# The last values made among attention's first scores, the exponentials' buffers moved, and a second norm queued behind the first turning

## The chip, the cores and the metric

The kernel runs on one core of a Trainium2 chip. A core has five engines that run side by side, each taking its own instructions in order: TensorE (PE; its weight loads are listed apart as PEld), VectorE (DVE), ScalarE (ACT), GpSimd (POOL) and SyncE (SP), which here only issues DMAs. They work on SBUF, 128 partitions of on-chip memory. TensorE writes to PSUM, eight banks of 128 partitions by 512 float32 values.

The metric is the time on the device, in microseconds, of one execution of the whole kernel. Times before and after are medians of several runs. A profile is one further execution, taken with the hardware profiler.

## The reference, cut to what matters

N = 4096 rows of width D = 256 pass through two layers. Layer 0 is a graph attention applied twice; layer 1, where all of the change lies, is a transformer block with 8 heads of 32 and a mask from `adj`:

```
# layer 0: two graph attentions with elu and residuals        (not touched)
# layer 1:
qkv    = layer_norm(x, g1, be1) @ w_qkv          # 4096 x 768: queries, keys, values
scores = einsum('nhd,mhd->hnm', q, k) * 32**-0.5
attn   = softmax(where(adj != 0, scores, -inf))
out    = einsum('hnm,mhd->nhd', attn, v).reshape(n, 256)
x      = x + out @ w_proj + b_proj
h2     = layer_norm(x, g2, be2)
x      = x + gelu(h2 @ w1 + b1) @ w2 + b2        # w1: 256 x 1024
```

## The kernel before, in words

Layer 1 is `unshifted_transformer`. It has three stages, and takes the rows in 8 blocks of 512 (`NB`), each of four tiles of 128 (`TB`).

**The projection** (lines 1782 to 1853, some 11.2 us per block) goes through the blocks `nb`. It transposes the next block's normed rows (L1556) and copies them out of PSUM with gain and bias (L1559); makes keys and then queries, two column tiles each (L1810); splits each result into a float16 head (the cast on ScalarE, L1817) and a float16 rest (the subtraction on VectorE, L1818) in a tile `u_halves`, which two DMAs store to `half_d` (L1822); and makes the block's values (L1829), which ScalarE copies to `u_v` (L1836). Then it loads keys of an earlier block from `half_d` into the layout that attention wants (L1734): the keys' heads go in twice and their rests twice, either all four by DMA (blocks from `NNB - 3` on) or two by DMA and two by a VectorE copy (L1846). The order of SP's queue is as written here; that of the other engines in this stage is made by a planner from the order of the program and its own estimates of when operands are ready. The SBUF pools `u_hv` (3 halves tiles) and `u_x` (5 tiles of rows) and a PSUM pool of all eight banks are opened for this stage. The weights `w_qkv` lie in `g_adj` tiles at the right end of SBUF, the normed and turned rows `g_ft` beside them; these two pools (stage and rows) are closed behind the projection (`pools.close()`).

**Attention** (lines 1876 to 2113) goes through 512 units (block of queries, group of four heads, tile of 128 keys), each in two steps `u` of two heads. A step's `weights` makes eight score matmuls into one of three two-bank PSUM tiles `u_ps` (L1872), the exponential in place on ScalarE (L1882), and the product with the mask on VectorE into `u_e` (L1883), one of ten buffers of the pool `u_work`. One step in 32 leaves the product to GpSimd. Two units later (`weigh`) TensorE multiplies the products with the values into `u_av`; GpSimd adds pairs of products into `u_both`, six more buffers of the same pool, and TensorE sums those four units later (`total`) into `u_dn`. These two are queued as parts in `waiting`, from which each step takes three or four behind its scores. Here all five engines' orders are as written: a stalled instruction holds everything behind it on its engine.

**The end of attention** is a table `ending`: by unit and step, what to do there. `project(k)` multiplies the first two blocks' attention with `w_proj` (L2048), adds it to the rows (L2056), takes the norm's moments (L1514, L1521, the root on ScalarE L1526), normalises (L1535, L1543) and adds `b2` on GpSimd (L2065). `turn_first(c)` transposes half of block 0's normed rows into `u_av` (L1556), and ScalarE copies them out (L1559).

**The feed-forward stage** goes through the eight blocks: 32 matmuls for `w1` (L2186) with Gelu on ScalarE (L2193), the projection of a later block (L2147), the next block's transposes, and 64 matmuls for `w2` (L2206). TensorE's order is as written.

A pool opened in the place of a closed one makes its first users wait until the closed pool's last users are done.

Of the kernel before, what the change touches and what calls it, by code (L numbers as in the profile page):

```python
# [22 lines left out]
P = 128  # L23
# [1544 lines left out]
class Ahead:  # L1568
# [26 lines left out]
    def normed(self, nb):  # L1595
        self.norms.normed(self.xs[nb], self.xs[nb], self.held.pop(nb))

    def turned(self, nb, c, pt):
        if c == 0:
            self.hn[nb] = self.stage_p.tile([P, self.D // P, 512], F32, name="g_ft", tag="stage")  # L1600
        self.norms.turned(self.hn[nb], c, self.xs[nb], pt, 1)

# [31 lines left out]
def unshifted_transformer(  # L1634
# [85 lines left out]
    with ExitStack() as scope:  # L1720
# [59 lines left out]
                load()  # L1780

        with ExitStack() as qkv:
            hv = qkv.enter_context(tc.tile_pool(name="u_hv", bufs=3))
            ps_q = qkv.enter_context(tc.tile_pool(name="u_ps_q", bufs=8, space=PSUM))
            u_x = qkv.enter_context(tc.tile_pool(name="u_x", bufs=5))
            wq_sb = ahead.w

            qkv.enter_context(tc.manual_schedule(engines={mybir.EngineType.SP}))
            for nb in range(3, 6):
                ahead.load(nb, u_x)  # L1790
            for nb in range(NNB):
                cols = slice(nb * NB, (nb + 1) * NB)
                hn = ahead.hn.pop(nb)
                if nb == 1:
                    for later_nb in range(6, NNB):
                        ahead.load(later_nb, u_x)
                if nb + 1 < NNB:
                    for c in range(DC):
                        ahead.turned(nb + 1, c, ps_q.tile([P, NB], F32, name="misc"))
                if 2 < nb + 2 < NNB:  # L1800
                    ahead.moments(nb + 2)
                    if nb + 3 == NNB:
                        nc.scalar.activation(rooted, ahead.held[nb + 2][:, 0, 1:2], AF.Exp)
                    ahead.normed(nb + 2)
                for i in (1, 0):
                    halves = hv.tile([P, 2, DC, NB], F16, name="u_halves")
                    for c in range(DC):
                        pq = ps_q.tile([P, NB], F32, name="misc")
                        for k in range(DC):
                            nc.tensor.matmul(  # L1810
                                pq,
                                wq_sb[k][:, i * D + c * P : i * D + (c + 1) * P],
                                hn[:, k, :],
                                start=(k == 0),
                                stop=(k == DC - 1),
                            )
                        nc.scalar.copy(halves[:, 0, c, :], pq)  # L1817
                        nc.vector.tensor_tensor(  # L1818
                            halves[:, 1, c, :], pq, halves[:, 0, c, :], op=ALU.subtract
                        )  # L1820
                    for kind in range(2):
                        nc.sync.dma_start(  # L1822
                            half_d[i, kind, :, :, cols].rearrange("c p n -> p c n"),
                            halves[:, kind],
                        )
                for t in range(TB):
                    pv = ps_q.tile([P, NB], F32, name="misc")
                    for k in range(DC):
                        nc.tensor.matmul(  # L1829
                            pv[:, :D],  # L1830
                            hn[:, k, t * P : (t + 1) * P],
                            wq_sb[k][:, 2 * D : 3 * D],
                            start=(k == 0),
                            stop=(k == DC - 1),
                        )
                    nc.scalar.copy(v_sb[:, nb * TB + t, :], pv[:, :D])  # L1836

                for b in (nb - 1,) if nb + 1 < NNB else (nb - 1, nb):
                    if b >= 0:
                        at = slice(b * NB, (b + 1) * NB)  # L1840
                        for c in range(DC):
                            late = b >= NNB - 3
                            kinds = (0, 0, 1, 1) if late else (0, None, 1, None)
                            stack(k_st[c][:, :, at], 1, kinds, at, c, HC)
                            for o in () if late else (0, 2 * O):
                                nc.vector.tensor_copy(  # L1846
                                    k_st[c][o + O : o + 2 * O, :, at], k_st[c][o : o + O, :, at]
                                )
                    if b == 0:
                        load_queries(0)  # L1850
                if 2 <= nb < 2 + NT // MC:
                    load_chunk(0, nb - 2)
        pools.close()


        work = scope.enter_context(tc.tile_pool(name="u_work", bufs=10))
        tail = scope.enter_context(tc.tile_pool(name="u_tail", bufs=1))
        ps_s = scope.enter_context(tc.tile_pool(name="u_ps_s", bufs=3, space=PSUM))
        ps_a = scope.enter_context(tc.tile_pool(name="u_ps_a", bufs=1, space=PSUM))
# [52 lines left out]
        def weigh(nb, c, mt, es, part):  # L1912
            if mt == 0 and part == 0:
                sums_of["av"] = ps_a.tile([P, NB], F32, name="u_av")
            h = c * HC
            lefts = [v_sb[:, mt, (h + j) * O : (h + j + 1) * O] for j in range(HC)]
            four(sums_of["av"], lefts, es, part, mt == 0, mt == NT - 1)
            if mt == NT - 1 and part == PARTS - 1:
                num = tail.tile([P, NB], F32, name="u_num", bufs=2)
                nc.scalar.copy(num, sums_of["av"])  # L1920
                nc.sync.dma_start(att_d[c, :, nb * NB : (nb + 1) * NB], num)

        def alone(mt):
            return mt // 2 % 8 == 7
# [89 lines left out]
        def rows_ready(k):  # L2014
# [8 lines left out]
                lambda: rows_ready(1),  # L2023
                lambda: nc.scalar.activation(rooted, norms.eps, AF.Sqrt),
                lambda: project(0),
            ],
            (last + 3, 0): [lambda: project(1)],
            (last + 3, 1): [lambda: turn_first(0)],
            (last + 4, 1): [lambda: turn_first(1)],
        }  # L2030

        def ready(step, i, es):
# [9 lines left out]
        def project(k):  # L2042
            res, att = early[k][:2]
            pp = ps_s.tile([P, 2, NB], F32, name="u_ps").rearrange("p a (b d) -> p (a b) d", d=D)
            per = TB // 2
            for t in range(TB):
                for c in range(DC):
                    nc.tensor.matmul(  # L2048
                        pp[:, t, :],
                        att[:, c, t * P : (t + 1) * P],  # L2050
                        early["wp"][:, c, :],
                        start=(t % per == 0 and c == 0),
                        stop=(t % per == per - 1 and c == DC - 1),
                    )
            for t in range(TB):
                nc.vector.tensor_tensor(res[:, t, :], res[:, t, :], pp[:, t, :], op=ALU.add)  # L2056
            both = norms.moments(res)
            if k == 0:
                two = blocks.tile([P, 2, TB * D], F32, name="u_q")
                res_n = two[:, 0].rearrange("p (t d) -> p t d", t=TB)  # L2060
                early["hn"] = two[:, 1].rearrange("p (c n) -> p c n", c=DC)
            else:
                res_n = masks.tile([P, TB, D], F32, name="u_mask")
            norms.normed(res_n, res, both)
            nc.gpsimd.tensor_tensor(  # L2065
                res, res, early["b2"].to_broadcast([P, TB, D]), op=ALU.add
            )
            early[k] = res, res_n

        def turn_first(c):  # L2070
            norms.turned(
                early["hn"], c, early[0][1], ps_a.tile([P, NB], F32, name="u_av"), 2
            )
        scope.enter_context(tc.manual_schedule(engines=ordered))
        for i in range(len(units) + 5):
            for u in range(HC // 2):
                if i < len(units):
# [8 lines left out]
                    if u == 0:  # L2086
                        pace()
                    es_of.setdefault(i, []).append(weights(*units[i], u))
                    if u == 0 and i + 2 < len(units) and units[i + 2][2] % 16 == 0 and (
                        units[i + 2] != (NNB - 1, DC - 1, NT // 2)  # L2090
                    ):
                        keep_mask(*units[i + 2])
                    if i % 2 == 1 and not alone(mt):
                        both = work.tile([P, 2, NB], F32, name="u_both", bufs=6)
                        nc.gpsimd.tensor_tensor(both, es_of[i - 1][u], es_of[i][u], op=ALU.add)  # L2095
                        both_of.setdefault(i, []).append(both)
                if u == 0 and 0 <= i - 2 < len(units):
# [18 lines left out]
    with ExitStack() as scope:  # L2116
# [43 lines left out]
        def turned(res_n):  # L2160
            hn = ln.tile([P, DC, NB], F32, name="ln_cols")
            for c in range(DC):
                norms.turned(hn, c, res_n, bank(), 2)
            return hn
# [162 lines left out]
```

## Time and profile before

| | |
|---|---|
| median of 3 runs | 3123.89 us (3123.82 to 3124.47) |
| the profiled execution | 3124.94 us on the device |
| its span, first to last instruction | 3123.2 us |
| mean granted TensorE clock | 0.995 of full |
| projection, first to last matmul | about 1601.7 to 1690.6 us of the span |
| attention, first score to last exponential | 1693.0 to 2850.8 us |
| feed-forward, from its first matmul | from 2865.9 us |

A page of the profile gives each engine's busy time, the chain of work that ended last (followed back from the end, from each instruction to what released it), and groups of instructions: line, engine, operation, output <- inputs, count, busy time and mean duration, and the idle time of the engine ahead of them with what ended it. Times of a timeline or chain are microseconds from the span's start. In a table by stretches, each engine has its busy microseconds and instruction count; the last three columns are the TensorE clock that was granted (1.00 is full), the DMA engines' busy share, and GB/s. Matmuls overlap, and the profile models their ends, so a busy TensorE need not be one at its peak.

### The profile page before, as it was taken

To read this page: it belongs to the slowest core of one execution; us is meant where nothing else is said; L and a number is where in the kernel's file an instruction comes from. 1 tells how busy PE (TensorE), PEld (TensorE's weight loads), DVE (VectorE), ACT (ScalarE), POOL (GpSimd) and SP (SyncE) were. 2 spreads that over 40 slices of the span, in tenths; PEclk is the share of its full clock that TensorE was granted. 3 is DMA by queue.
4 is the path that set the end of the run, shared out by engine and by line. 5 is a ranking of instruction groups with operands and counts; after the bars stand their busy time and mean duration, and the time that the engine had idled before them with its cause. 6 is when DMAs were issued, how large, how long until landed. Compare 5 with 4: busy or idle time off the path is not lost.

```text
span 3123.2 us, 139201 instructions
## 1 busy us (share of the span) xinstructions
PE 3061.6 (98%) x63976; PEld 2713.3 (87%) x63976; DVE 2747.7 (88%) x3110; ACT 2699.7 (86%) x3370; POOL 1265.1 (41%) x568
## 2 busy tenths in 40 slices
PE   6999999999999999999999999999999999999998
PEld 5899999999889999999975888888888888887766
DVE  7999999999989999999985999999999999997220
ACT  6899999999899999999975999999999999996232
POOL 3300000000330000000002999999999999997110
PEclk8999999999999999999999999999999999999999
DMA  8666555431311213121145101010101110013210
GB/s 257 218 198 205 171 174 167 144 100 33 91 59 29 90 56 97 32 64 53 46 116 152 34 21 35 21 41 28 35 21 35 30 30 28 28 40 102 68 34 22
DMA packets 213171, 250.35 MB, mean 80 GB/s; under 512 B 89120, under 2 KB 133664, under 8 KB 212576
## 3 DMA queue, kind: packets, MB, share of 16 engines
q1 hardware_dynamic: 212576, 241.37, 25.1%
q8 instruction: 502, 8.22, 1.1%
q14 instruction: 93, 0.76, 0.1%
HBM read 198.84 MB, written 42.47 MB: 77 GB/s over the span
## 4 chain that ended last, share of the span: by engine, by line
PE 51%; ACT 1%; DVE 1%; issue 0%; DMA 0%; DVEq 0%; ACTq 0%
PE u_ps L1872 15%; PE u_av L1904 14%; PE u_dn L1904 8%; PE misc L2186 4%; PE misc L2206 4%; PE bank L1463 3%; PE misc L1810 2%; PE misc L1829 1%; ACT t L1122 1%; PE misc L2147 1%; PE misc L1556 0%; DVE t L1137 0%; DVE t L1124 0%; DVE u_e L1883 0%; PE u_ps L2048 0%
## 5 line engine op out<-in xcount | busy, mean ns | idle before, releaser
L1463 PE MATMUL bank<-vst,t 128*128 128x132 f16 x16384 | 1455.9, 220 | 3.6 <-DVE t L1137 2.7
L2095 POOL TENSOR_TENSOR u_both<-u_e 128x1024 f32<-128x1024 f32 x448 | 1047.9, 2388 | 805.1 <-DMA u_k<-half_d 775.6
L1463 PE MATMUL bank<-vst,mask 128*128 128x132 f16 (+1 forms) x10516 | 1372.3, 206 | 0.0
L1122 ACT ACTIVATE t<-s_b,g_terms 128x1024 int8<-128x1024 f32 x1234 | 1318.7, 1148 | 21.0 <-PE bank L1463 15.2
L1463 PEld LDWEIGHTS <-t 128*128 128x128 fp8e4 x16384 | 1186.3, 96 | 15.8 <-DVE t L1137 5.4
L1883 DVE SCALAR_TENSOR_TENSOR u_e<-u_mask,u_ps 128x1024 f32<-128x1024 uint8 x994 | 1131.5, 1213 | 26.8 <-ACT u_ps L1882 25.8
L1882 ACT ACTIVATE u_ps<-u_ps 128x1024 f32<-128x1024 f32 x994 | 996.4, 1008 | 93.0 <-PE u_ps L1872 33.6
L1463 PEld LDWEIGHTS <-mask 128*128 128x128 fp8e4 x10516 | 920.4, 98 | 0.0
L1137 DVE SCALAR_TENSOR_TENSOR t<-mask,t 128x2048 int32<-128x2048 int32 x256 | 587.9, 2296 | 74.8 <-ACT t L1122 66.4
L1872 PE MATMUL u_ps<-u_q,u_k 128*32 128x512 f16 x8192 | 632.4, 381 | 7.0 <-DVE u_e L1883 4.5
L1904 PE MATMUL u_av<-u_e,u_v 128*32 128x128 f32 x16384 | 602.9, 273 | 0.0
L1124 DVE TENSOR_SCALAR t<-s_b,g_terms 128x1024 fp8e4<-128x1024 f32 x814 | 590.1, 758 | 2.7 <-DMA s_b<-s_d 2.7
L1904 PEld LDWEIGHTS u_av<-u_e,u_v 128*32 128x32 f32 x16384 | 483.2, 110 | 120.6 <-issue 0.7
L1054 POOL TENSOR_TENSOR vst<-g_adj,vst 128x528 f16<-128x528 f32 x16 | 19.9, 1241 | 725.7 <-ACT g_big L1018 681.6
L1904 PE MATMUL u_dn<-u_both,u_ones 128*32 128x128 f32 x7168 | 279.2, 273 | 0.0
L1904 PEld LDWEIGHTS u_dn<-u_both,u_ones 128*32 128x32 f32 x7168 | 212.9, 110 | 52.1 <-issue 0.7
L1872 PEld LDWEIGHTS <-u_k 128*32 128x32 f16 x8192 | 229.5, 96 | 29.2 <-issue 8.9
L2193 ACT ACTIVATE u_hid<-misc,n_b 128x512 f32<-128x512 f32 x64 | 43.9, 687 | 140.3 <-PE misc L2186 140.3
L2206 PE MATMUL misc<-u_k,u_hid 128*128 128x256 f32 x512 | 111.8, 379 | 0.0
L2206 PEld LDWEIGHTS misc<-u_k,u_hid 128*128 128x128 f32 x512 | 96.7, 190 | 13.3 <-issue 0.5
L2186 PE MATMUL misc<-ln_cols,u_k 128*128 128x512 f32 x224 | 97.3, 592 | 0.0
L867 DVE TENSOR_SCALAR adj<-g_adj 128x1024 fp8e4<-128x1024 int32 x123 | 88.9, 723 | 3.8 <-DMA g_adj<-in_adj_dram 3.8
(186 smaller groups left out, 1919.2 us busy)
## 6 DMA issues: line engine op xcount, KB each, us to landing
g_adj<-in_adj_dram SPq DMA_DIRECT2D x123, 512.0 KB
s_b<-s_d SPq DMA_DIRECT2D x64, 512.0 KB
mask<-mask SPq DMA_DIRECT2D x128, 256.0 KB
u_mask<-mask SPq DMA_DIRECT2D x64, 256.0 KB
mask<-stage SPq DMA_DIRECT2D x48, 256.0 KB
half_d<-u_halves SPq DMA_DIRECT2D x32, 256.0 KB
u_q<-half_d SPq DMA_DIRECT2D x32, 256.0 KB
rows<-e_x SPq DMA_DIRECT2D x31, 256.0 KB
```

Of the source, the lines that this page charges most:

```text
L867: nc.vector.tensor_scalar(v.rearrange("p m r -> p r m"), loaded.pop((nb, c, i)), 1.0, -(2.0**-30), op0=ALU.min, op1=ALU.max, saturate=False,)
L1122: nc.scalar.activation(to.bitcast(I8), s, AF.Sign, bias=negd, scale=-1.0)
L1124: nc.vector.tensor_scalar(to, s, negd, -1.0, op0=ALU.is_ge, op1=ALU.mult, saturate=False)
L1137: nc.vector.scalar_tensor_tensor(both, m32.unsqueeze(1).to_broadcast(list(both.shape)), SIGNS, both, op0=ALU.bitwise_or, op1=ALU.bitwise_and,)
L1463: nc.tensor.matmul(to, left, right, start=k not in opened, stop=last)
L1872: nc.tensor.matmul(ps[r * O : (r + 1) * O, j, :], k_st[c][:, 2 * u + j, at : at + O], q_st[:, h, :], start=True, stop=True,)
L1882: nc.scalar.activation(ps, ps, AF.Exp, scale=SCALE)
L1883: nc.vector.scalar_tensor_tensor(e, mask, 0.0, ps, op0=ALU.not_equal, op1=ALU.mult)
L1904: nc.tensor.matmul(to[j * O : (j + 1) * O, at], lefts[j], es[j // 2][:, j % 2, at], start=first and part == 0, stop=last and part == PARTS ...
L2095: nc.gpsimd.tensor_tensor(both, es_of[i - 1][u], es_of[i][u], op=ALU.add)
L2186: nc.tensor.matmul(ph, w1_sb[:, k, f * P : (f + 1) * P], hn[:, k, :], start=(k == 0), stop=(k == DC - 1),)
L2206: nc.tensor.matmul(po[:, :D], hid[:, f, at : at + P], w2_sb[:, f, :], start=(f == 0), stop=(f == FC - 1),)
```

## The change

Six edits, all in layer 1:

- Block 7's values are not made in the projection. Its turned rows go to a new tile `hn_last` and a copy of the values' weights to `wv_last`, both parts of one buffer of the pool `u_blocks` (`spare`). A new function `last_values(t)` makes them at attention's steps 2 (t = 0, 1, 2) and 4 (t = 3), in the two banks of `u_av` and `u_dn`; ScalarE copies two tiles at a time to `u_v`.
- The projection's eight banks become pools of six and two. The last block's keys use the six, its queries the two; the scores' tiles come to lie on the six, `u_av` and `u_dn` on the two.
- `u_hv` has four buffers for three.
- The pool `u_work` goes to the right end of SBUF, over the closed pools of old rows; the sums `u_both` get a pool of their own on the left, `u_adds`.
- Block 4's keys too are loaded four times by DMA (`NNB - 4`), without VectorE copies.
- `project` is cut in two: the norm is now `norm_rows`. For block 0 it follows at once as before; for block 1 it stands behind the second `turn_first`.

```diff
-    def turned(self, nb, c, pt):
-        if c == 0:
+    def turned(self, nb, c, pt, to=None):
+        if to is not None:
+            self.hn[nb] = to
+        elif c == 0:
             self.hn[nb] = self.stage_p.tile([P, self.D // P, 512], F32, name="g_ft", tag="stage")
...
-            hv = qkv.enter_context(tc.tile_pool(name="u_hv", bufs=3))
-            ps_q = qkv.enter_context(tc.tile_pool(name="u_ps_q", bufs=8, space=PSUM))
+            hv = qkv.enter_context(tc.tile_pool(name="u_hv", bufs=4))
+            psums = [
+                qkv.enter_context(tc.tile_pool(name=f"u_ps_q{k}", bufs=n, space=PSUM))
+                for k, n in enumerate((6, 2))
+            ]
+            used = []
+
+            def bank(which=None):
+                used.append(None)
+                k = len(used) % 4 == 0 if which is None else which
+                return psums[k].tile([P, NB], F32, name="misc")
+
             u_x = qkv.enter_context(tc.tile_pool(name="u_x", bufs=5))
             wq_sb = ahead.w
+            spare = blocks.tile([P, 4 * NB], F32, name="u_q")
+            hn_last = spare[:, : DC * NB].rearrange("p (c n) -> p c n", c=DC)
+            wv_last = spare[:, DC * NB : DC * NB + DC * D].rearrange("p (c e) -> p c e", c=DC)
...
-                        ahead.turned(nb + 1, c, ps_q.tile([P, NB], F32, name="misc"))
+                        to = hn_last if nb + 2 == NNB else None
+                        ahead.turned(nb + 1, c, bank(), to)
+                if nb == 3:
+                    for c in range(DC):
+                        nc.sync.dma_start(
+                            wv_last[:, c], ahead.w_qkv[c * P : (c + 1) * P, 2 * D : 3 * D]
+                        )
...
-                        pq = ps_q.tile([P, NB], F32, name="misc")
+                        pq = bank(1 - i if nb + 1 == NNB else None)
...
-                for t in range(TB):
-                    pv = ps_q.tile([P, NB], F32, name="misc")
+                for t in range(TB) if nb + 1 < NNB else ():
+                    pv = bank()
...
-                            late = b >= NNB - 3
+                            late = b >= NNB - 4
...
-        work = scope.enter_context(tc.tile_pool(name="u_work", bufs=10))
+        work = scope.enter_context(tc.tile_pool(name="u_work", bufs=10, side="right"))
+        adds = scope.enter_context(tc.tile_pool(name="u_adds", bufs=6))
...
+        def last_values(t):
+
+            at, name = (NNB - 1) * TB + t // 2 * 2, ("u_av", "u_dn")[t // 2]
+            if t % 2 == 0:
+                sums_of[name] = ps_a.tile([P, NB], F32, name=name)
+            to = sums_of[name]
+            for k in range(DC):
+                nc.tensor.matmul(
+                    to[:, t % 2 * D : (t % 2 + 1) * D],
+                    hn_last[:, k, t * P : (t + 1) * P],
+                    wv_last[:, k, :],
+                    start=(t % 2 == 0 and k == 0),
+                    stop=(t % 2 == 1 and k == DC - 1),
+                )
+            if t % 2 == 1:
+                nc.scalar.copy(
+                    v_sb[:, at : at + 2, :].rearrange("p t d -> p (t d)"), sums_of.pop(name)
+                )
...
                 lambda: project(0),
+                lambda: norm_rows(0),
             ],
             (last + 3, 0): [lambda: project(1)],
             (last + 3, 1): [lambda: turn_first(0)],
-            (last + 4, 1): [lambda: turn_first(1)],
+            (last + 4, 1): [lambda: turn_first(1), lambda: norm_rows(1)],
...
                 nc.vector.tensor_tensor(res[:, t, :], res[:, t, :], pp[:, t, :], op=ALU.add)
+
+        def norm_rows(k):
+            res = early[k][0]
             both = norms.moments(res)
...
                     es_of.setdefault(i, []).append(weights(*units[i], u))
+                    for t in {2: (0, 1, 2), 4: (3,)}.get(2 * i + u, ()):
+                        last_values(t)
...
-                        both = work.tile([P, 2, NB], F32, name="u_both", bufs=6)
+                        both = adds.tile([P, 2, NB], F32, name="u_both")
```

## The prediction

> **What bounds the kernel now.** The profiled execution took 3124.94 us on the device; its span is 3123.2 us, 0.7 us under the median of the timed runs (3123.89), so I sum in the span's own clock and subtract the result from the median. The page comes first:
>
> ```profile
> PE 3061.6 (98%) x63976; PEld 2713.3 (87%) x63976; DVE 2747.7 (88%) x3110; ACT 2699.7 (86%) x3370; POOL 1265.1 (41%) x568
> L1883 DVE SCALAR_TENSOR_TENSOR u_e<-u_mask,u_ps 128x1024 f32<-128x1024 uint8 x994 | 1131.5, 1213 | 26.8 <-ACT u_ps L1882 25.8
> L1872 PE MATMUL u_ps<-u_q,u_k 128*32 128x512 f16 x8192 | 632.4, 381 | 7.0 <-DVE u_e L1883 4.5
> ```
>
> TensorE looks like the bound, but its ends are modelled. The timeline of VectorE (start, length, instruction) says more of attention:
>
> ```profile
> 1696.62 5.76 DVE L1883 SCALAR_TENSOR_TENSOR u_e<-u_mask,u_ps 128x1024 f32<-128x1024 uint8 x5 [3.84 <-ACT u_ps L1882]
> 1703.10 30.63 DVE L1883 SCALAR_TENSOR_TENSOR u_e<-u_mask,u_ps 128x1024 f32<-128x1024 uint8 x27 [0.72 <-ACT u_ps L1882]
> 1734.44 35.22 DVE L1883 SCALAR_TENSOR_TENSOR u_e<-u_mask,u_ps 128x1024 f32<-128x1024 uint8 x31 [0.71 <-ACT u_ps L1882]
> ```
>
> From 1703 on it rests only 0.7 us per 32 steps (a step is half a unit), at the product that GpSimd makes. Its pace is 35.22/31 = 1.136 us, or 9.09 us per 8 steps; TensorE's chain needs 9.05 for the same 8. With every score at its shortest, 0.43, TensorE would need 8 x 0.43 + 4 x 0.87 (values) + 2 x 0.87 (sums) = 8.7. So VectorE paces attention, and TensorE has some 0.4 us per 8 steps in hand. What counts at the start is when VectorE makes its first product. The chain there:
>
> ```profile
> 1692.10 0.69 DVE u_halves L1818
> ...
> 1692.81 3.69 DMA half_d<-u_halves
> ...
> 1696.62 2.36 DVE u_e L1883 x2
> ```
>
> The first product stands on the memory of `u_halves` and waits until the last halves have been stored. The timelines of TensorE and ScalarE show why these are late:
>
> ```profile
> 1686.94 3.62 PE L1829 MATMUL misc<-g_adj,g_ft 128*128 128x256 f32 x16
> 1692.99 1.48 PE L1872 MATMUL u_ps<-u_q,u_k 128*32 128x512 f16 x24 [2.43 <-issue]
> 1690.60 0.37 ACT L1836 COPY u_v<-misc 128x256 f32<-128x256 f32 x1 [0.49 <-PE misc L1829]
> 1690.87 1.08 ACT L1817 CAST u_halves<-misc 128x512 f16<-128x512 f32 x2
> 1693.65 2.84 ACT L1882 ACTIVATE u_ps<-u_ps 128x1024 f32<-128x1024 f32 x3 [1.70 <-PE u_ps L1872]
> ```
>
> The queries' casts follow the last copy of values, though their matmuls had ended at 1687.1. At attention's end the timeline of ScalarE, the chain, and the table by stretches (last columns: granted clock, DMA) read:
>
> ```profile
> 2864.24 0.30 ACT L1526 ACTIVATE n_mean<-n_mean,n_eps 128x4 f32<-128x4 f32 x1 [6.35 <-DVE n_mean L1521]
> 2864.45 0.76 ACT L1559 ACTIVATE u_q<-u_av,n_be,n_g 128x512 f32<-128x512 f32 x1
> 2865.11 0.57 ACT L1937 COPY u_den<-u_dn 128x512 f32<-128x512 f32 x1
> 2866.12 0.78 ACT L1559 ACTIVATE u_q<-u_av,n_be,n_g 128x512 f32<-128x512 f32 x1 [0.44 <-PE u_av L1556]
> ```
>
> ```profile
> 2866.09 15.26 PE misc L2186 x32
> 2899.49 13.73 PE misc L2186 x32
> ```
>
> ```profile
> 2864.00:2866.00 2.00, 0.74 (x5) 0.74 (x6) 1.60 (x9) 1.44 (x3) 0.00 (x0) 0.91 0.48 129
> 2866.00:2868.00 2.00, 2.00 (x4) 0.84 (x4) 0.17 (x1) 0.78 (x1) 1.68 (x1) 0.50 1.08 393
> 2868.00:2870.00 2.00, 2.00 (x4) 0.72 (x3) 0.00 (x0) 0.59 (x1) 2.00 (x2) 0.74 0.48 137
> ```
>
> The first turning (2864.45) was ready when its transposes ended at 2862.49, but stands behind the second block's root; TensorE idles 1.99 us, its clock halves, and the first 32 feed-forward matmuls take 15.26 instead of 13.73. After them TensorE is continuous to the end.
>
> **What the Trainium skill says.** "TensorE: Matmul & The Clock Gate", Part 1: the array drops to half clock after an idle window of about 3.4 us and returns after a busy one. The trace agrees on rate and length (0.50, then 0.74, then 1.00), though the listed idle was only 1.99 us. The same page, "Architectural detail", calls ScalarE's and VectorE's queues strictly first in, first out; the root holding a ready turning shows it. "DMA: Bandwidth & Descriptors", "Anatomy of one DMA", gives about 2.0 us fixed per transfer; the halves' store took 3.69, which I use. "SBUF — State Buffer", "SBUF: two separate sides", lets VectorE and GpSimd contend when a VectorE operation reads two SBUF operands; L1883 reads one and PSUM, so where `u_e` lies should not matter.
>
> **The change, part by part.** (a) Block 7's 8 value matmuls (3.47 us) and 4 copies leave their place. TensorE ends the queries at 1687.11, and scores 0 to 2 may follow at once: their six banks were last read by the keys' VectorE subtraction (1685.0), since the queries now use the other two. ScalarE: query casts 1685.4 and 1687.15 to 1687.73; first exponential from 1687.75, 0.95 long (2.84/3). VectorE: subtraction to 1688.46; first product at about 1688.8. Its buffers now lie over old rows and weights, last read by TensorE at 1687.1, so no transfer holds it. Gain against 1696.62: 7.8 us.
>
> (b) Step 2 adds 3 x 0.87 us on TensorE, which waits for the queries' subtraction (1688.5, a wait of 0.1) and ends at 1691.1; behind it stand score 3 and then all of attention's matmuls. Score 3 could have gone at 1690.0 when VectorE freed its bank. ScalarE then copies two tiles (512 columns, 0.57) before exponential 3: it runs 1691.8 to 1692.8. VectorE ends its third product at 1692.25 and begins the fourth at 1692.85: gap 0.6. Step 4 adds 0.87 and a copy to 1694.35; exponential 5 ends 1695.35, product 4 at 1695.15: gap 0.25. After that each score is released more than one exponential ahead. Before there was one gap of 0.72 (1702.38 to 1703.10), so this costs 0.85 - 0.72 = 0.13. The moved 3.47 us fill TensorE's idle of that stretch (2.43 + 3.43 + 1.1 later). Were the idle already full, they would cost up to 3.47, repaid from the 0.4 per 8 steps.
>
> (c) Block 4's keys: 4 VectorE copies (4 x 0.685, at 1685.05 to 1687.88) go; kept, they would stand before the queries' subtraction, about 0.5 us. Four more loads at 0.48 us of issue each (1.93/4), and two value-weight loads on the same queue at 0.36 to 0.5 (unseen as such; nearest rows are the other issues), are hidden: that queue had some 3 us free before block 3's stores and waited 32.6 us for casts. Uncovered they would cost 2.9 us. Blocks 6 and 7's keys land near 1702 and are read from unit 24, 54 us after the start.
>
> (d) Four halves buffers instead of three let query casts go before value copies: nothing in the earlier blocks, where TensorE is continuous. `u_both` on the old halves waits for their store, 1688.5 + 3.69 = 1692.2; its data come at 1692.25. Free.
>
> (e) The second norm: 4 statistics, 4 aggregates, root, reciprocal, 4 normalisations, one GpSimd addition, no DMA. VectorE's order stays. On ScalarE the root passes two turnings and the denominators' copy, and their four den_d stores on SP go out earlier. First turning 2862.53 to 2863.29, copy to 2863.88, transposes 2863.33 to 2864.15, second turning 2864.19 instead of 2866.12: 1.93 us. TensorE's idle falls to about 0.2, so the clock should hold: 15.26 - 13.73 = 1.53 more. Late next is the root, at 2864.97 (0.7 later), which leaves Gelu's table load free at 2865.3, before its data; normalisation and the addition end near 2869.3, while TensorE wants those rows at about 2881.
>
> Sum: 7.8 - 0.1 + 1.9 + 1.5 = 11.1 us; 3123.9 - 11.1 = 3112.8. The unseen terms: gap cost 0.13, from -0.7 to +1.5; clock relief 0 to 1.6.
>
> **Rivals.** *Clock still falls at the end* (free-running window, fp32 transposes counting as little work): 3114.3. For it: only 1.99 us of idle sufficed before. *The store still gates the first product* because some buffer meets the halves: then it starts at 1692.3, gain 4.3 + 3.4, 3116.2. Against: `u_work` starts 40 KB below the right end, and the 32 KB of sums and tail fit left of it, so it begins at least 16 KB past the four halves tiles. *The front gain doesn't come*: ScalarE's order in the projection is the planner's, and query casts or their banks stay late by 5 to 8 us; only the end is won, 3120.4. Against: before, no exponential went ahead of a cast. *Slower*: VectorE, without slack, makes its products more slowly at the new addresses. 994 x 11.2 ns (0.9% of 1213) cancel the gain; 17.5 ns make it slower by over 0.2%; at 20 ns it is 3123.9 - 11.1 + 19.9 = 3132.7. Against: ten old buffers gave 1157 to 1223 ns, median 1212.
>
> **How the numbers follow.** Forecast 0.62; clock 0.14; store 0.08; no front gain 0.07; slower 0.05; still faster than the forecast's range (fewer gaps) 0.04. No change can be told within 0.2%, 6.25 us: faster is below 3117.6. The first three and the last give 0.88, of which I leave 0.01 to same: faster 0.87, same 0.08, slower 0.05. The forecast's own range is 3110.5 to 3114; with the clock and store cases it reaches 3117.
>
> **What would show it.** First product near 1689, with gaps of about 0.6 and 0.25 on VectorE and none by a DMA; no half clock at 1696 to 1702; values' matmuls amid the first scores. At the end the root after both turnings, the first L2186 group near 13.7 and no clock of 0.50. Wrong if the product's mean leaves 1213 ns, if a transfer stands before the first product, or if ScalarE runs exponentials before query casts.

## The result, and the profile after

The kernel after takes 3114.65 us (median of 8 runs, 3113.41 to 3115.09), the kernel before 3123.86 beside it (8 runs, 3123.18 to 3126.1): 9.2 us less, a ratio of 0.9969 with a 95% interval of 0.9958 to 0.998. The profiled execution after took 3114.7 us, its span 3112.9, against 3123.2 before. So the spans differ by 10.3 us, 1.1 more than the medians; the profiled execution of before was 1.1 over its median.

The page of the kernel after, lines as shown of before:

```profile
PE 3059.2 (98%) x63976; PEld 2711.5 (87%) x63976; DVE 2749.2 (88%) x3106; ACT 2701.0 (87%) x3368; POOL 1266.7 (41%) x568
L1905 DVE SCALAR_TENSOR_TENSOR u_e<-u_mask,u_ps 128x1024 f32<-128x1024 uint8 x994 | 1131.8, 1211 | 23.7 <-ACT u_ps L1904 22.4
L1894 PE MATMUL u_ps<-u_q,u_k 128*32 128x512 f16 x8192 | 631.5, 380 | 0.7 <-DVE u_e L1905 0.7
```

No engine's busy time tells of the gain: TensorE's fell by 2.4 us, VectorE's rose by 1.5. The product with the mask has kept its mean (1211 ns, 1213 before), and TensorE stands idle ahead of the scores for 0.7 us in all, in place of 7.0. VectorE's timeline at attention's start:

```profile
1688.99 3.48 DVE L1905 SCALAR_TENSOR_TENSOR u_e<-u_mask,u_ps 128x1024 f32<-128x1024 uint8 x3 [0.29 <-ACT u_ps L1904]
1693.26 2.35 DVE L1905 SCALAR_TENSOR_TENSOR u_e<-u_mask,u_ps 128x1024 f32<-128x1024 uint8 x2 [0.78 <-ACT u_ps L1904]
1695.96 30.76 DVE L1905 SCALAR_TENSOR_TENSOR u_e<-u_mask,u_ps 128x1024 f32<-128x1024 uint8 x27 [0.35 <-ACT u_ps L1904]
```

The first product begins at 1688.99 instead of 1696.62, behind an exponential and no DMA. Two gaps follow, 0.78 and 0.35, where before had one of 0.72. ScalarE and the chain show what makes them:

```profile
1687.39 0.59 ACT L1838 CAST u_halves<-misc 128x512 f16<-128x512 f32 x1 [1.13 <-PE misc L1831]
1687.95 2.84 ACT L1904 ACTIVATE u_ps<-u_ps 128x1024 f32<-128x1024 f32 x3
1690.79 0.59 ACT L1960 COPY u_v<-u_av 128x512 f32<-128x512 f32 x1
1692.21 1.93 ACT L1904 ACTIVATE u_ps<-u_ps 128x1024 f32<-128x1024 f32 x2 [0.84 <-PE u_ps L1894]
```

```profile
1687.36 1.41 PE u_ps L1894 x24
1688.77 1.99 PE u_av L1952 x8
1690.75 0.86 PE u_dn L1952 x4
1691.62 0.98 PE u_ps L1894 x16
1692.59 1.06 PE u_dn L1952 x4
```

The last query cast ends where the first exponential begins. Three value tiles stand between scores 2 and 3, and after its copy ScalarE still waits 0.84 us for score 3. At attention's end, ScalarE, the chain, and the table by stretches:

```profile
2855.70 0.78 ACT L1559 ACTIVATE u_q<-u_av,n_be,n_g 128x512 f32<-128x512 f32 x1 [4.63 <-PE u_av L1556]
2856.57 0.59 ACT L1978 COPY u_den<-u_dn 128x512 f32<-128x512 f32 x1
2857.23 0.78 ACT L1559 ACTIVATE u_q<-u_av,n_be,n_g 128x512 f32<-128x512 f32 x1
2857.91 0.29 ACT L1526 ACTIVATE n_mean<-n_mean,n_eps 128x4 f32<-128x4 f32 x1
```

```profile
2857.19 0.86 PE misc L2233 x2
2858.06 13.14 PE misc L2233 x30
```

```profile
2858.00:2860.00 2.00, 1.99 (x6) 0.98 (x6) 1.74 (x4) 0.93 (x3) 0.99 (x1) 1.00 1.02 352
```

The root stands behind both turnings, TensorE has no listed idle there, its clock stays at 1.00, and the first 32 feed-forward matmuls take 14.0 us instead of 15.26.

**A measure finer than the median.** The projection's first transpose comes at 1600.40 to 1603.27 us in the profiles of before, after and the twelve experiments, though no edit touches anything before it. That moves whole times by up to 2.9 us, as much as many of the edits. So I count from that transpose, in three segments: A to the first product, B from there to the end of the last product, C from there to the end of the first 32 feed-forward matmuls. In code that an edit leaves alone, A agrees within 0.4 us (before, e1 and e4) or 0.01 (after, e2, e8 and e13), B within 0.4, C within 0.02.

| kernel | A | B | C | sum | against before | median, us |
|---|---|---|---|---|---|---|
| before | 94.97 | 1155.67 | 29.06 | 1279.70 | | 3123.86 |
| after | 87.09 | 1156.48 | 25.74 | 1269.31 | -10.39 | 3114.65 |
| e1_norm_only | 95.35 | 1155.99 | 25.73 | 1277.07 | -2.63 | 3121.55 |
| e2_front_only | 87.10 | 1156.75 | 29.05 | 1272.90 | -6.80 | 3117.60 |
| e3_left_place | 91.74 | 1157.56 | 25.73 | 1275.03 | -4.67 | 3119.29 |
| e4_filler | 95.36 | 1155.68 | 27.64 | 1278.68 | -1.02 | 3122.77 |
| e5_no_values | 87.10 | 1155.15 | 25.73 | 1267.98 | -11.72 | 3113.01 |
| e7_one_psum | 88.56 | 1156.40 | 25.74 | 1270.70 | -9.00 | 3115.86 |
| e8_values_spread | 87.09 | 1156.55 | 25.73 | 1269.37 | -10.33 | 3114.44 |
| e9_key_copies | 87.10 | 1156.61 | 25.73 | 1269.44 | -10.26 | 3114.02 |
| e10_three_halves | 87.09 | 1163.53 | 25.74 | 1276.36 | -3.34 | 3121.29 |
| e11_place_only | 93.04 | 1154.89 | 29.04 | 1276.97 | -2.73 | 3121.49 |
| e12_values_stay | 91.13 | 1156.26 | 25.73 | 1273.12 | -6.58 | 3117.51 |
| e13_values_345 | 87.10 | 1156.56 | 25.73 | 1269.39 | -10.31 | 3114.29 |

Of the 10.39 us, A gives 7.88, C 3.32, and B takes back 0.81. Each row's segments come from one profiled execution. The medians of the experiments were taken beside other executions of before than the 3123.86 of the first row: its median was 3124.48 with e1 to e4 (46 runs), 3124.55 with e5, e7, e8 and e11 (26 runs) and 3123.89 with the rest (35 runs). So a difference of two medians of this column can be off by some 0.7 us.

### The profile page after: what moved, and what is told of

The parts are those of the page before. It is cut to its first block, busy times and chain, and to the rows that moved or that the text cites. A ratio compares the mean times of both kernels' runs of the same rounds, so it can differ in the third digit from the quotient of the medians.

```text
span 3112.9 us, 139205 instructions
## 1 busy us (share of the span) xinstructions
PE 3059.2 (98%) x63976; PEld 2711.5 (87%) x63976; DVE 2749.2 (88%) x3106; ACT 2701.0 (87%) x3368; POOL 1266.7 (41%) x568
## 4 chain that ended last, share of the span: by engine, by line
PE 51%; ACT 1%; DVE 1%; issue 0%; DVEq 0%; ACTq 0%
PE u_ps L1894 15%; PE u_av L1926 14%; PE u_dn L1926 8%; PE misc L2253 4%; PE misc L2233 4%; PE bank L1463 3%; PE misc L1831 2%; ACT t L1122 1%; PE misc L1850 1%; PE misc L2194 1%; PE misc L1556 0%; DVE t L1137 0%; PE u_ps L2090 0%; DVE t L1124 0%; DVE u_e L1905 0%
## 5 line engine op out<-in xcount | busy, mean ns | idle before, releaser
L1905 DVE SCALAR_TENSOR_TENSOR u_e<-u_mask,u_ps 128x1024 f32<-128x1024 uint8 x994 | 1131.8, 1211 | 23.7 <-ACT u_ps L1904 22.4
```

Source lines behind the costliest of these rows:

```text
L1905: nc.vector.scalar_tensor_tensor(e, mask, 0.0, ps, op0=ALU.not_equal, op1=ALU.mult)
```

## The experiments

### The two ends apart: the norm alone, the front alone

On the kernel before, only the norm is moved; on the kernel after, only the norm is put back.

```diff
                 lambda: project(0),
+                lambda: norm_rows(0),
...
-            (last + 4, 1): [lambda: turn_first(1)],
+            (last + 4, 1): [lambda: turn_first(1), lambda: norm_rows(1)],
...
+        def norm_rows(k):
+            res = early[k][0]
...
```

> The kernel before with the second norm alone moved behind both turnings. My theory: the turning goes ahead of the root, which saves 1.9 to 2.1 us, and TensorE then idles too briefly for its clock to fall, 1.5 more: 3.3 to 3.6 us in all, first group of 32 feed-forward matmuls 13.7 to 14.2 us, clock 1.00 there. Rival (clock falls all the same): 1.9 us, and the group stays near 15.3.

```diff
-            (last + 3, 0): [lambda: project(1)],
+            (last + 3, 0): [lambda: project(1), lambda: norm_rows(1)],
...
-            (last + 4, 1): [lambda: turn_first(1), lambda: norm_rows(1)],
+            (last + 4, 1): [lambda: turn_first(1)],
```

> The changed kernel with the second norm back in its old place. My theory: the gain of attention's start alone, 6.5 to 7.2 us against the kernel before; at the end TensorE idles some 2 us again and the first feed-forward group takes about 15.3 us. Rival (the two gains share a cause, or the start's gain is lost again by the end of attention): less than 5 us.

Segment C is 25.73 with the norm alone and 29.05 with the front alone; A is 95.35 and 87.10. The ratios to before are 0.9991 (0.9984 to 0.9998) and 0.9977 (0.9968 to 0.9987). The chain of the front alone, and its stretch at that place:

```profile
2858.76 15.16 PE misc L2233 x32
```

```profile
2858.00:2860.00 2.00, 2.00 (x6) 1.19 (x6) 0.75 (x3) 1.04 (x2) 1.54 (x1) 0.52 0.72 262
```

The half clock and the long group are back, with the whole front gain kept. The two gains lie each in its own segment. Added, they give 9.43 of the 10.39 us; the rest is of the size of the scatter of A and B.

### How much of the end is the clock: TensorE's idle filled, the order left

On the kernel before, two matmuls of no use go ahead of the second half's turning, into a free score tile. ScalarE's order stays as before.

```diff
-            (last + 4, 1): [lambda: turn_first(1)],
+            (last + 4, 1): [lambda: filler(), lambda: turn_first(1)],
...
+        def filler():
+            pp = ps_s.tile([P, 2, NB], F32, name="u_ps")
+            for j in range(2):
+                nc.tensor.matmul(pp[:, j, :], early["w1"][:, j, :P], early["w1"][:, j, :NB], start=True, stop=True)
```

> The kernel before with two more fp32 matmuls of 128x512 (1.7 us of TensorE, results unused) between the last sums and the second turning's transposes, where TensorE idled 1.99 us. My theory: nothing waits longer, the clock doesn't fall, and the first feed-forward group takes 13.7 to 14.3 us: 1.2 to 1.6 us faster than the kernel before. Rival (the group's 15.3 us come from waits for its operands, not from the clock): no gain, or up to 0.5 us slower.

The chain shows the filler and the first group:

```profile
2865.30 1.07 PE u_ps L2073 x2
...
2867.94 0.86 PE misc L2197 x2
2868.81 13.14 PE misc L2197 x30
```

The group takes 14.0 us, as in the kernel after, and the clock at 2868 to 2870 is 1.00. C falls by 1.42 although TensorE does more work. Of the 3.33 us of the moved norm alone, then, some 1.4 is the clock and the other 1.9 the order. The whole time can't show 1.4 us here (3122.77, ratio 0.9996, 0.9987 to 1.0005); the segment does.

### The place of the exponentials' buffers

On the kernel after, the pool goes back to the left, over the old halves.

```diff
-        work = scope.enter_context(tc.tile_pool(name="u_work", bufs=10, side="right"))
-        adds = scope.enter_context(tc.tile_pool(name="u_adds", bufs=6))
+        work = scope.enter_context(tc.tile_pool(name="u_work", bufs=10))
...
-                        both = adds.tile([P, 2, NB], F32, name="u_both")
+                        both = work.tile([P, 2, NB], F32, name="u_both", bufs=6)
```

> The changed kernel with products and sums in one pool on the left again, over the halves. My theory: the first product waits for the last halves' store, which now lands near 1692.3, so it starts 3.3 us later than in the changed kernel; the two gaps behind it (1.13 us) shrink to some 0.3 to 0.7, since scores have more time: 2.5 to 3.0 us slower than the changed kernel. Rival (the place is of no account, the queries' earlier casts did it all): within 0.3 us of it.

It is 5.72 us slower than the kernel after by segments, 4.6 by medians: the sign held, the size did not. VectorE and then TensorE:

```profile
1692.78 5.75 DVE L1904 SCALAR_TENSOR_TENSOR u_e<-u_mask,u_ps 128x1024 f32<-128x1024 uint8 x5 [4.93 <-DMA u_k<-half_d]
1700.75 30.63 DVE L1904 SCALAR_TENSOR_TENSOR u_e<-u_mask,u_ps 128x1024 f32<-128x1024 uint8 x27 [2.23 <-ACT u_ps L1903]
```

```profile
1694.05 0.62 PE L1893 MATMUL u_ps<-u_q,u_k 128*32 128x512 f16 x8 [3.29 <-DVE u_e L1904]
...
1696.02 2.07 PE L1951 MATMUL u_dn<-u_q 128*128 128x256 f32 x4
```

The first product waits for a transfer and comes 4.65 us later in A, not 3.3. The chain there names the store:

```profile
1687.87 4.42 DMA half_d<-u_halves
...
1692.78 2.36 DVE u_e L1904 x2
```

(The timeline puts the wait down to `u_k`, the chain to `u_halves`; VectorE waits for several transfers here, and both views only infer which came last.) The store was sized at the 3.69 us of before and took 4.42, and VectorE began 0.49 us after its end, where before it took 0.12. The store's length varies without any edit: in e1 and e4, which leave this part as in before, it took 4.07 and 4.09 us. Why it does is open. And TensorE, with no products, idles 3.29 us; the stretch 1696 to 1698 has a clock of 0.50, the last value tile takes 2.07 us instead of 1.13, and a gap of 2.23 opens.

On the kernel before, the place alone is changed.

```diff
-        work = scope.enter_context(tc.tile_pool(name="u_work", bufs=10))
+        work = scope.enter_context(tc.tile_pool(name="u_work", bufs=10, side="right"))
+        adds = scope.enter_context(tc.tile_pool(name="u_adds", bufs=6))
...
-                        both = work.tile([P, 2, NB], F32, name="u_both", bufs=6)
+                        both = adds.tile([P, 2, NB], F32, name="u_both")
```

> The kernel before with u_work at the right end and u_both in u_adds on the left, and nothing else. My theory (two gates in a row: behind the store stands the late cast of the queries): the first product moves only from 95.0 us after the projection's first transpose to about 93.0, when the first exponential of the late scores is done, so 1.7 to 2.2 us faster than the kernel before. Rival (the parts simply add: the place is worth what the changed kernel loses without it): 4.5 us or more.

```profile
1694.02 36.28 DVE L1884 SCALAR_TENSOR_TENSOR u_e<-u_mask,u_ps 128x1024 f32<-128x1024 uint8 x32 [1.91 <-ACT u_ps L1883]
```

A falls by 1.93, and B by 0.78, since the gap of 0.72 is gone. That is 2.73 us, more than the 1.7 to 2.2 looked for by the gap, where the same edit taken out of the kernel after costs 5.72. The medians (3121.49 beside 3124.55) agree on the small size. Behind the store stood another gate: the queries' casts, at 1690.19 in this kernel, which counted from the first transpose is as late as in before. They stand behind the value copies, the subtraction and the first score (1692.31) follow them, and no product can be earlier. The gates stand in series, and the place is worth its full amount only when the values are out of the way.

### The moved values

On the kernel after, `last_values` returns at once, which prices the whole of the moved work where it now lies.

```diff
+            nc.gpsimd.memset(v_sb[:, (NNB - 1) * TB :, :], 0.0)
...
         def last_values(t):
...
+            return
...
```

> The changed kernel without the last block's values: last_values does nothing, and GpSimd fills those 512 rows of u_v with zeros during the projection (so the output lacks their part). My theory (VectorE paces attention, the moved matmuls lie in TensorE's idle time): the two gaps behind the first products, 0.78 and 0.35 us, close, and no more: 0.7 to 1.2 us faster than the changed kernel, from the start of the projection to the last product. Rival (TensorE is the bound, moved work costs its own length): 3.5 us faster.

```profile
1688.11 36.41 DVE L1906 SCALAR_TENSOR_TENSOR u_e<-u_mask,u_ps 128x1024 f32<-128x1024 uint8 x32 [0.29 <-ACT u_ps L1905]
```

All 32 products run without a gap. TensorE is relieved of 3.91 us of matmuls (1.99, 0.86 and 1.06 in the chain of after) and B falls by only 1.33, just over the 0.7 to 1.2 looked for and far from the rival's 3.5; 1.13 of it are the two gaps. So VectorE paces attention, and the values cost their gaps, not their matmuls.

Can they be placed better? In two kernels on after they are spread over other steps.

```diff
-                    for t in {2: (0, 1, 2), 4: (3,)}.get(2 * i + u, ()):
+                    for t in {2: (0, 1), 7: (2,), 9: (3,)}.get(2 * i + u, ()):
```

> The changed kernel with the last values at steps 2 (t = 0, 1), 7 (t = 2) and 9 (t = 3) instead of 2 (t = 0, 1, 2) and 4 (t = 3). My theory (the 0.78 us gap is score 3 standing behind three value tiles): the first gap closes to 0.1 or less, 0.1 to 0.4 us stays elsewhere, so the last product comes 0.5 to 1.0 us earlier. Rival (the gap is ScalarE's copy, not the score): the gaps keep their sum of 1.1 us.

```diff
-                    for t in {2: (0, 1, 2), 4: (3,)}.get(2 * i + u, ()):
+                    for t in {2: (0, 1), 3: (2,), 5: (3,)}.get(2 * i + u, ()):
```

> The changed kernel with the last values at steps 2 (t = 0, 1), 3 (t = 2) and 5 (t = 3). My theory: TensorE has some 3 us of idle up to step 11 and the tiles take 4, so about 0.7 to 1.1 us of gaps on VectorE stay wherever they stand; from first to last product 1156.0 to 1156.5. Rival (there is a placing without gaps): 1155.2.

The first of them, on VectorE:

```profile
1688.29 9.14 DVE L1905 SCALAR_TENSOR_TENSOR u_e<-u_mask,u_ps 128x1024 f32<-128x1024 uint8 x8 [0.29 <-ACT u_ps L1904]
1697.58 2.35 DVE L1905 SCALAR_TENSOR_TENSOR u_e<-u_mask,u_ps 128x1024 f32<-128x1024 uint8 x2 [0.15 <-ACT u_ps L1904]
1700.58 7.03 DVE L1905 SCALAR_TENSOR_TENSOR u_e<-u_mask,u_ps 128x1024 f32<-128x1024 uint8 x6 [0.64 <-ACT u_ps L1904]
```

The early gaps are gone, and new ones open behind the later tiles: 0.15, 0.64 and one of 0.29 further on, 1.08 in all where after has 1.13. B is 1156.55 against 1156.48; the hoped-for gain did not come, and the rival's sum of 1.1 us held, though not its reason: ScalarE's copy stands as early as before and the gap behind it is gone. The second has gaps of 0.38 and 0.57, and B is 1156.56, beside the 1156.0 to 1156.5 looked for. Three placings give the same sum within 0.1 us. Without the values TensorE rests some 2.95 us up to step 11, and the tiles want 3.9: about 1 us has to come out somewhere.

Last, on the kernel after the values go back to the projection, with everything else as it is.

```diff
-                for t in range(TB) if nb + 1 < NNB else ():
-                    pv = bank()
+                for t in range(TB):
+                    pv = bank(0 if nb + 1 == NNB else None)
...
-                    for t in {2: (0, 1, 2), 4: (3,)}.get(2 * i + u, ()):
+                    for t in {}.get(2 * i + u, ()):
```

> The changed kernel with the last block's values made in the projection again (from the six banks), all else as changed. My theory: the scores wait for the last value copy, some 3.6 us, so the first product comes about 91.0 us after the projection's first transpose instead of 87.1; the gaps behind the first products vanish, which gives 1.6 back: 2.0 to 2.6 us slower than the changed kernel. Rival (the move saves its whole length): 3.5 us or more slower.

A rises by 4.04, B falls by 0.22: 3.81 slower by segments, 2.9 by medians. I had looked for 2.0 to 2.6; by segments the rival's 3.5 or more held, by medians neither. VectorE and the table by stretches:

```profile
1693.27 5.76 DVE L1905 SCALAR_TENSOR_TENSOR u_e<-u_mask,u_ps 128x1024 f32<-128x1024 uint8 x5 [4.32 <-ACT u_ps L1904]
1699.94 30.76 DVE L1905 SCALAR_TENSOR_TENSOR u_e<-u_mask,u_ps 128x1024 f32<-128x1024 uint8 x27 [0.91 <-ACT u_ps L1904]
```

```profile
1696.00:1698.00 2.00, 2.00 (x36) 1.64 (x32) 2.00 (x3) 1.22 (x2) 1.12 (x1) 0.50 1.00 211
```

The gaps were to vanish with the tiles; one of 0.91 stands there. TensorE, with nothing to do beside the first scores, idles 1.55 and 0.51 us and its clock falls to 0.50. In the kernel after the moved tiles fill that idle, and no stretch there is below 1.00. But idle does not decide it alone: with the place alone (e11), and without the values (e5), TensorE idled 1.50 and 0.52 us at the same scores and kept 1.00 in every stretch. So in part these 3.81 us, like the 5.72 of the left place, may be the chance of one execution; by the medians both are about 1 us less.

### PSUM, keys and the fourth halves tile

Each of the three small edits is undone by itself on the kernel after. First, one pool of eight banks:

```diff
-                for k, n in enumerate((6, 2))
+                for k, n in enumerate((8,))
...
-                return psums[k].tile([P, NB], F32, name="misc")
+                return psums[0].tile([P, NB], F32, name="misc")
```

> The changed kernel with one pool of eight PSUM banks for the projection, keys and queries in turn. My theory: the first score then waits for the last subtraction of the queries, 1.4 us later than in the changed kernel, and the first product with it: 1.2 to 1.5 us slower. Rival (a score waits only for its own banks' last readers, so nothing changes): within 0.3 us.

TensorE's timeline:

```profile
1688.84 1.48 PE L1894 MATMUL u_ps<-u_q,u_k 128*32 128x512 f16 x24 [1.40 <-DVE u_halves L1839]
```

The first scores wait 1.40 us for the queries' subtraction, and A grows by 1.47. This went as expected.

Second, block 4's keys copied by VectorE again:

```diff
-                            late = b >= NNB - 4
+                            late = b >= NNB - 3
```

> The changed kernel with block 4's keys copied by VectorE again. My theory: of the four copies of 0.685 us two or more stand around the queries' last subtraction and ahead of the first product, which comes 0.5 to 1.4 us later; from there nothing changes: 0.5 to 1.4 us slower. Rival (they fit into VectorE's idle time between the subtractions): within 0.2 us.

```profile
1687.50 1.22 DVE L1905 SCALAR_TENSOR_TENSOR u_e<-u_mask,u_ps 128x1024 f32<-128x1024 uint8 x1 [0.29 <-ACT u_ps L1904]
1688.75 0.68 DVE L1867 COPY u_k<-u_k 32x2048 f16<-32x2048 f16 x1
1689.46 1.22 DVE L1905 SCALAR_TENSOR_TENSOR u_e<-u_mask,u_ps 128x1024 f32<-128x1024 uint8 x1
```

A is the same, the sum 0.13 us longer. Two of the four copies fall between the subtractions and two between the first products, in time that VectorE would have spent in the gaps of 0.78 and 0.35, which are gone. The theory that they cost 0.5 us or more falls and the rival's size held; this edit is worth nothing here.

Third, three halves tiles instead of four:

```diff
-            hv = qkv.enter_context(tc.tile_pool(name="u_hv", bufs=4))
+            hv = qkv.enter_context(tc.tile_pool(name="u_hv", bufs=3))
```

> The changed kernel with three halves tiles. My theory: in the last block there are no value copies for the casts to stand behind, so the first product comes at the same time: within 0.3 us of the changed kernel. Rival (the fourth tile is what makes the queries' casts early): 2 us or more slower, with the casts of the last queries late.

It is 7.05 us slower than the kernel after (6.6 by medians), as the rival had it, and nearly all of the front gain is gone. ScalarE, TensorE and VectorE:

```profile
1688.61 2.84 ACT L1904 ACTIVATE u_ps<-u_ps 128x1024 f32<-128x1024 f32 x3 [3.41 <-PE u_ps L1894]
1691.34 1.10 ACT L1838 CAST u_halves<-misc 128x512 f16<-128x512 f32 x2
1698.23 0.58 ACT L1960 COPY u_v<-u_av 128x512 f32<-128x512 f32 x1 [5.78 <-PE u_av L1952]
```

```profile
1694.44 3.75 PE L1952 MATMUL u_av<-u_q 128*128 128x256 f32 x8 [5.01 <-issue]
```

```profile
1700.97 2.35 DVE L1905 SCALAR_TENSOR_TENSOR u_e<-u_mask,u_ps 128x1024 f32<-128x1024 uint8 x2 [6.63 <-ACT u_ps L1904]
```

The first three exponentials stand ahead of the last two query casts. ScalarE waits 3.41 us for scores 0 to 2, which begin at 1687.95, right behind the queries' matmuls. The first of the queries' two tiles was ready some 1.7 us before (an estimate: the 16 matmuls that make four such tiles took 6.87 us). ScalarE casts both at 1691.34, and VectorE subtracts them, behind its first three products, up to 1694.3. Only then may the values take those two banks, and TensorE, with nothing to do for 5.01 us, runs them at half the clock (0.50 from 1692 to 1698): 3.75 us for two tiles instead of 1.99. A gap of 6.63 us follows. The first product is as early as in the kernel after, A being 87.09, so looking at the first product alone one would not have seen the loss. That the planner, with three buffers, holds the casts due after the exponentials is inferred from the order that it made; its own estimates are in no trace.

## Why the prediction was right, and where it wasn't

**The mechanism held at both ends, the size nearly.** 3114.65 us stands 1.9 above the forecast of 3112.8. That is 0.65 above the forecast's own range of 3110.5 to 3114, and inside the 3117 which that range reached only with the clock and store cases. Neither of these came about, so that the wider range took in the result is luck. The sum of steps said 11.1; the segments give 10.39, which would have been 3113.5, in the forecast's own range, and the medians 9.2. The last 1.2 us between segments and medians are not settled; the scatter ahead of the projection is more than enough for them.

**(a) held.** 7.88 us against 7.8. The first product is at 1688.99 (1688.8 forecast) and stands behind no transfer. e3, e7 and e12 show that the store, the banks and the values each were a gate: undone singly they cost 5.7, 1.4 and 3.8 us. Together with the halves tile's 7.05 this is 18 us for a gain of 7.07 (A and B), which is what gates in series look like: such prices can't be added. A part of the 5.7, 3.8 and 7.05 is also half clock, as those three profiles show.

**(b) is the mis-sized term.** The working gave 0.13 us of loss; B rose by 0.81. The gaps came to 1.13 instead of 0.85, which explains 0.41 against before's 0.72. The three tiles at step 2 kept score 3 back until 1691.62 (1691.1 forecast), and ScalarE had no work for 0.84 us. The value tiles took 3.91 us, not 3.47. The other 0.40 lies spread over 1156 us and is as large as B's scatter in unchanged code. The claim that TensorE's idle absorbs the tiles held: e5 gets back 1.33 us for 3.91 us of matmuls. To the clock in that stretch the step gave no price, though it was 0.57 at 1698 to 1700 in the kernel before; it fell to 0.50 in e3 and e12, and not in e5 and e11.

**(c) was wrong, and cost nothing.** The 0.5 us for kept copies would not have been lost: e9 finds 0.13, because VectorE's idle time takes them in. The prediction put the copies ahead of the queries' last subtraction; two of them went there without delaying it, and the other two behind it, into the gaps that (b) had forecast itself.

**(d) was wrong.** The fourth halves tile got no price in the sum. That is right for its cost, but undone it costs 7.05 us: the tile is what lets the query casts stand ahead of the exponentials, so that (a) came true through an edit whose worth was put at nothing. The rival in which ScalarE's order spoils the front stood one buffer away, and its counter-argument (that no exponential went ahead of a cast in the kernel before) was no proof, since three tiles with the other edits do just that. It gave 3120.4; e10 measured 3121.29.

**(e) held.** C fell by 3.32 against 3.46; e4 puts 1.4 of it down to the clock (1.53 forecast) and leaves 1.9 to the order (1.93). The rival in which the clock still falls did not occur: 1.00 at 2858 to 2860. The Trainium skill, "TensorE: Matmul & The Clock Gate", Part 1, speaks of an idle window of about 3.4 us. As in the kernel before, e12 had half a clock behind less listed idle (1.55 and 0.51 us), and e11 and e5, with 1.50 and 0.52, had none. The page also calls the window free-running, so that equal idle may or may not bring the clock down; these three profiles agree with that and do not prove it. At the end three profiles without the moved norm and without the filler (before, e2, e11) give C as 29.04 to 29.06, so there the fall was no chance.

**The slower rival is refuted.** It needed the product's mean to rise by 17.5 ns; it fell by 2. The store's rival did not come true: no transfer stands before the first product. e3, which undoes that edit, measured 3119.29, worse than the 3116.2 worked out for it: the store was longer, and the clock fell.

## What to carry to other kernels

Where several waits stand in series, price an edit by taking it out of the finished kernel and by putting it alone into the old one; here one and the same edit was worth 5.7 and 2.7 us. An edit that looks as if it cost and brought nothing, such as one more buffer, can decide the order that a planner gives an in-order engine, so look at that order up to the last instruction that the next stage waits for, and not only at its first result. Work moved off a path into an engine's idle time was paid here in the gaps of the engine that sets the pace (1.1 us for 3.9 us of matmuls), so its price is read there and not from its own length.

## What the runs showed of the hardware

In the kernel after, VectorE's four normalisations of the second block took 3.41 us, where the same four took 1.38 before, and the little operation on `u_inside` 1.69 instead of 0.23:

```profile
2858.44 3.41 DVE L1543 TENSOR_SCALAR u_mask<-u_q,n_mean 128x256 f32<-128x256 f32 x4
...
2862.81 1.69 DVE L2220 TENSOR_SCALAR u_inside<-u_dens 128x256 f32<-128x256 f32 x1
```

Both ran beside additions on GpSimd that lie between SBUF tiles (2859.01 to 2861.38 and 2862.00 to 2864.35); in the kernel before the additions came after the normalisations, from 2866.32. The new place of the norm is not the cause: in e1, e3, e5 and e12 it has that place, no addition began before the last of the four normalisations, and they took 1.38. In all six profiles in which one did (after, e7, e8, e9, e10, e13) they took 3.41 to 3.50. The operation on `u_inside` ended 0.15 us behind the addition beside it, in the kernel after and in e12 (1.42 us) alike. The Trainium skill, "SBUF — State Buffer", "SBUF: two separate sides", gives VectorE and GpSimd one shared pair of ports, held by one of them for a whole instruction; the traces agree with a block of this kind, though no edit was made to try it. The prediction took from that section only operations with two SBUF operands; the section also names VectorE operations in a two-port mode, and those slowed here read one tile. It cost nothing: C is 25.73 or 25.74 with the block and without it.
